# Fetching the first adjacency block in two row groups, and the attention rows in three transfers

## The chip, the core and the metric

The kernel runs on one core of a Trainium2 chip. The core has a matrix engine (TensorE, PE in the profile), VectorE (DVE), ScalarE (ACT), GpSimd (POOL) and SyncE (SP), and 16 DMA engines that move data between the chip's memory and the on-chip buffer. The metric is the device time of one execution in microseconds. The profile that is quoted was taken from one execution; its span runs from the first to the last instruction of the core.

## The reference

The reference is one graph-attention layer with a residual and a layer norm. `x` is 4096 x 512, `adj` is 4096 x 4096, `W` is 512 x 2048 (four heads of 512), `a` holds two vectors of 512 for each head, all in float32.

```
ht      = (x @ W) split into 4 heads
e       = leaky_relu(src_i + dst_j) + adj_ij        # for each head
h_prime = mean over heads of softmax(e) @ ht
out     = layernorm(x + h_prime)
```

`adj` is added as it stands, and its entries reach 1e9. So in almost every row the softmax puts all its weight on the column where `adj` is largest, and `h_prime` of that row is `x[column] @ mean over heads of W`. The kernel computes that, and tests with a bound from the norms of `x`, `W` and `a` that the largest entry leads far enough; rows where it doesn't are done by a general path, which isn't entered for these inputs.

## The kernel before, in words

The 4096 rows are handled as NB = 32 blocks of 128 rows, P = 128 being the number of partitions. Block `ib` holds rows `32*p + ib`, so partition `p` of a block gets one row of 16 KB (4096 floats), and neighbouring partitions read rows that lie 512 KB apart in memory. All of this is in `leading_rows`.

For each block VectorE takes maxima over short segments (`segment_maxima`, L180), finds the leading segment (L187, L189), and GpSimd fetches that segment again with an indirect DMA (L200). Two blocks later VectorE finds the column in it (L217, L223), and GpSimd gathers the row of `x` that belongs to it (L211). Three blocks after the first step TensorE turns this row (L238) and multiplies it by the mean of the heads' weights (L253), adding `x` through an identity matmul (L246). ScalarE takes the statistics and scales (L275, L277, L286), and SP stores.

The order of all instructions is written out by hand (`tc.manual_schedule`). Every large transfer is issued from SP, in program order, on one queue: block 0 of `adj`, half of `W`, block 1, the other half of `W`, blocks 2 to 4, the first rows of `x`. From then on the loop over `t` issues the load of block `t + 5`. The adjacency blocks live in a pool of six buffers (`AHEAD + 1`), so a later load also waits until VectorE has left the buffer of six blocks before.

The four small transfers of `a` (L135) are issued from ScalarE, in front of its first other work. They bring the eight attention vectors, of 2 KB each, to partitions 0 to 7, two rows each time. TensorE turns them (L353) after the first weight blocks have been averaged.

Transfers from SP and ScalarE take turns on eight completion semaphores, which are called lanes here (0 to 7). A transfer that gets a lane waits until the lane's last transfer has landed. Before, the lanes of the first eight transfers are: rows of `a` 0, 2, 3 and 4; block 0 of `adj` 1; first half of `W` 5; block 1 of `adj` 6; second half of `W` 7. So block 2 of `adj` waits for the first transfer of `a`, block 3 for block 0 of `adj`, block 4 and the first rows of `x` for the second and third transfers of `a`, and block 5 for the fourth.

Of the kernel before, what the change touches and what calls it, by code (L numbers as in the profile page):

```python
# [9 lines left out]
F32 = mybir.dt.float32  # L10
# [10 lines left out]
P = 128  # L21
# [9 lines left out]
def gat_resnorm_kernel(  # L31
# [29 lines left out]
    any_bad = keep.tile([1, 1], I32, name="any_bad")  # L61

    leading_rows(tc, x, adj, W, a, out, ident, v, n_bad, any_bad)

    flag = nc.values_load(any_bad[0:1, 0:1], min_val=0, max_val=N)
# [5 lines left out]
def leading_rows(ctx, tc, x, adj, W, a, out, ident, v, n_bad, any_bad):  # L71
# [8 lines left out]
    nc = tc.nc  # L80
    N, D = x.shape
    H = a.shape[0]
# [8 lines left out]
    adj_pool = ctx.enter_context(tc.tile_pool(name="adj_pool", bufs=AHEAD + 1))  # L91
# [7 lines left out]
    adj_rows = adj.rearrange("(p nb) m -> nb p m", nb=NB)  # L99
# [11 lines left out]
    a_rows = once.tile([2 * H, D], F32, name="a_rows")  # L111

    once.tile([P, 32], F32, name="pad_end")
    adj_t = {}

    def pieces(ib):
        return PIECES if ib == NB - 1 else 2 if ib >= LATE else 1

    def load_adj(ib):
        if 0 <= ib < NB:  # L120
            t = adj_t[ib] = adj_pool.tile([P, N], F32, name="adj_t")
            n = pieces(ib)
            for k in range(n):
                nc.sync.dma_start(t[:, ts(k, N // n)], adj_rows[ib][:, ts(k, N // n)])  # L124
# [4 lines left out]
    def load_w(kb, n):  # L129
        nc.sync.dma_start(hold[:, ds(w_at + kb * H, n * H), :], w_blocks[:, ds(kb * H, n * H), :])  # L130

    load_adj(0)
    for s in range(2):
        for h in range(0, H, H // 2):
            nc.scalar.dma_start(  # L135
                a_rows[ds(s * H + h, H // 2), :], a[ds(h, H // 2), ts(s, D), :].rearrange("h d o -> h (d o)")
            )
    for kb in range(0, KB, 2):
        load_w(kb, 2)
        load_adj(kb // 2 + 1)  # L140
# [291 lines left out]
    for t in range(NB):  # L432
# [29 lines left out]
        ib = t - PROJECT  # L462
# [244 lines left out]
```

## Time and profile before

| what | value |
|---|---|
| time, median of 3 runs | 235.2 us (234.88 to 235.32) |
| time of the profiled execution | 234.9 us |
| its span | 233.4 us |
| PE busy | 199.9 us (86%) |
| DVE busy | 191.3 us (82%) |
| ACT busy | 111.8 us (48%) |
| POOL busy | 100.7 us (43%) |
| bytes moved by DMA | 97.12 MB, mean 416 GB/s |
| granted TensorE clock, mean | 0.965 |

Busy time is the time in which an engine executed something; PE and DVE overlap for most of the span. The DMA share is the mean busy share of the 16 DMA engines. The time of an execution lies 1.5 us above its span. Beside the views the trace has a record of every DMA packet, with its queue, start, duration and size; packets of 16,384 bytes are rows of an adjacency block. Where a packet's time is given below, it comes from these records, counted from the span's start.

### The profile page before, as it was taken

How to read it: one execution, taken by the hardware profiler on the slowest of the kernel's cores; microseconds unless marked ns; L12 is line 12 of the kernel's file. 1: busy time of each engine (PE TensorE's matmuls, PEld its weight loads, DVE VectorE, ACT ScalarE, POOL GpSimd, SP SyncE). 2: the span in 40 equal slices, each digit the busy share in tenths (PEclk: the TensorE clock that was granted, in tenths of full speed). 3: DMA queues.
4: the chain of work that ended last, by engine and by line, in shares of the span. 5: the costliest groups of instructions: out<-in, count | busy, mean ns of one | idle time of the engine just before them, and what ended most of it. 6: DMA issues, size and time to landing. Idle time of an engine off the chain costs nothing.

```text
span 233.4 us, 2484 instructions
## 1 busy us (share of the span) xinstructions
PE 199.9 (86%) x683; PEld 105.3 (45%) x683; DVE 191.3 (82%) x300; ACT 111.8 (48%) x267; POOL 100.7 (43%) x215
## 2 busy tenths in 40 slices
PE   0069995999999999999999779879998977999980
PEld 0034644646565555665645244334443433444460
DVE  0548299689929999999788995999999999998881
ACT  2001223014474757575767455545664644188561
POOL 2020234414524464644543452647464564548300
PEclk9999999579999999999999979999999999999997
DMA  6999999999999999999999999999999999999995
GB/s 237 423 432 428 428 438 426 415 439 436 422 421 437 423 431 425 431 419 428 430 430 428 432 423 432 423 430 421 426 433 420 426 423 426 412 424 420 421 414 213
DMA packets 12257, 97.12 MB, mean 416 GB/s; under 512 B 1992, under 2 KB 2440, under 8 KB 6480
## 3 DMA queue, kind: packets, MB, share of 16 engines
q1 hardware_dynamic: 8640, 88.08, 89.1%
q0 software_dynamic: 3584, 8.84, 9.6%
q8 instruction: 6, 0.10, 0.2%
q14 instruction: 11, 0.09, 0.1%
q10 hardware_dynamic: 16, 0.02, 0.0%
HBM read 88.54 MB, written 8.39 MB: 415 GB/s over the span
## 4 chain that ended last, share of the span: by engine, by line
DMA 64%; DVE 21%; PE 11%; SPq 1%; issue 1%; ACT 0%; DVEq 0%
DMA adj_t<-in_adj_dram 53%; DVE seg L180 17%; DMA hold<-in_x_dram 11%; PE o L253 6%; PE o L295 2%; DVE at L189 1%; PE tp L238 1%; DVE top L187 1%; PE o L246 1%; DVE within L223 1%; SPq L130 1%; PE o L291 0%; SPq L124 0%; DVE inner L217 0%; ACT hold L335 0%
## 5 line engine op out<-in xcount | busy, mean ns | idle before, releaser
L180 DVE TENSOR_REDUCE seg<-adj_t 128x128 f32<-128x2048 f32 (+3 forms) x66 | 145.5, 2208 | 28.5 <-DMA adj_t<-in_adj_dram 28.2
L253 PE MATMUL o<-w_sum,yt 128*128 128x512 f32 x248 | 117.6, 616 | 0.7 <-ACT yt L240 0.7
L253 PEld LDWEIGHTS o<-w_sum,yt 128*128 128x128 f32 x248 | 45.6, 196 | 55.2 <-issue 43.9
L240 ACT COPY yt<-tp 128x512 f32<-128x512 f32 x32 | 18.8, 588 | 43.9 <-PE tp L238 43.8
L200 POOL DMA_INDIRECT lead<-in_adj_dram,row x32 | 32.3, 1008 | 14.6 <-POOL row L196 14.6
L211 POOL DMA_INDIRECT y<-in_x_dram,col x32 | 30.9, 964 | 15.4 <-POOL col L225 15.1
L238 PE MATMUL tp<-ident,y 128*128 128x128 f32 x128 | 22.1, 296 | 10.2 <-DMA y<-in_x_dram,col 10.1
L246 PE MATMUL o<-hold,ident 128*128 128x512 f32 x52 | 28.5, 634 | 1.7 <-DMA hold<-in_x_dram 1.7
L343 PE MATMUL o<-hold,ident 128*128 128x512 f32 x32 | 17.3, 696 | 13.6 <-DMA hold<-in_L_gnn_W_dram 13.6
L238 PEld LDWEIGHTS tp<-ident,y 128*128 128x128 f32 x128 | 18.5, 209 | 22.8 <-issue 20.5
L361 ACT COPY wt<-tp 128x512 f32<-128x512 f32 x16 | 9.2, 587 | 38.2 <-PE tp L359 38.2
L196 POOL TENSOR_TENSOR row<-at,first 128x1 uint32<-128x1 uint32 x32 | 6.1, 190 | 43.6 <-DVE at L189 43.6
L367 PEld LDWEIGHTS pv<-at_d,wt 128*128 128x128 f32 x128 | 17.2, 200 | 7.4 <-ACT wt L361 3.7
L260 ACT ACTIVATE sq<-hold 128x512 f32<-128x512 f32 x32 | 19.8, 620 | 0.0
L225 POOL TENSOR_TENSOR col<-start,within 128x1 uint32<-128x1 uint32 x31 | 5.9, 190 | 32.2 <-DVE within L223 32.2
L286 ACT ACTIVATE hold<-o,nm,sd 128x512 f32<-128x512 f32 x24 | 17.2, 771 | 0.0
L277 ACT ACTIVATE sq<-o,nm 128x512 f32<-128x512 f32 x24 | 16.5, 687 | 0.8
L343 PEld LDWEIGHTS o<-hold,ident 128*128 128x128 f32 x32 | 6.9, 225 | 21.5 <-issue 21.5
L367 PE MATMUL pv<-at_d,wt 128*128 128x2 f32 x128 | 16.0, 249 | 0.6 <-ACT wt L361 0.6
L344 ACT ACTIVATE w_sum<-o 128x512 f32<-128x512 f32 x4 | 2.4, 598 | 27.5 <-PE o L343 27.5
L275 ACT ACTIVATE sq<-o 128x512 f32<-128x512 f32 x24 | 14.5, 606 | 0.0
L187 DVE MAX8 top<-seg 128x8 f32<-128x256 f32 (+2 forms) x32 | 11.6, 362 | 1.1
(86 smaller groups left out, 140.0 us busy)
## 6 DMA issues: line engine op xcount, KB each, us to landing
adj_t<-in_adj_dram SPq DMA_DIRECT2D x28, 2048.0 KB, 30.8
adj_t<-in_adj_dram SPq DMA_DIRECT2D x6, 1024.0 KB, 28.1
hold<-in_L_gnn_W_dram SPq DMA_DIRECT2D x2, 2048.0 KB, 16.4
hold<-in_x_dram SPq DMA_DIRECT2D x2, 2048.0 KB, 37.6
out_dram<-hold SPq DMA_DIRECT2D x4, 1024.0 KB, 16.1
out_dram<-hold SPq DMA_DIRECT2D x7, 512.0 KB, 14.4
hold<-in_x_dram SPq DMA_DIRECT2D x3, 1024.0 KB
adj_t<-in_adj_dram SPq DMA_DIRECT2D x4, 512.0 KB, 19.8
```

What stands on the lines that cost most here:

```text
L180: nc.vector.tensor_reduce(seg_of[ib][:, ts(k, N // e // n)], adj_t[ib][:, ts(k, N // n)].rearrange("p (s e) -> p s e", e=e), axis=AX.X, op ...
L200: nc.gpsimd.indirect_dma_start(out=lead, out_offset=None, in_=adj_segs[e], in_offset=bass.IndirectOffsetOnAxis(ap=row[:, :1], axis=0),)
L211: nc.gpsimd.indirect_dma_start(out=y, out_offset=None, in_=x, in_offset=bass.IndirectOffsetOnAxis(ap=col[:, :1], axis=0),)
L238: nc.tensor.transpose(tp[:, kb, :], y[:, ds(kb, P, KB)], ident)
L240: nc.scalar.copy(yt, tp)
L246: nc.tensor.matmul(o_ps[ib], ident, hold[:, ib, :], start=start, stop=False)
L253: nc.tensor.matmul(o_ps[ib], yt_of[ib][:, kb, :], w_sum[:, kb, :], start=(start and kb == 0), stop=(kb == KB - 1),)
L260: nc.scalar.activation(sq, hold[:, ib, :], AF.Square, accum_out=xx[:, ib : ib + 1])
L277: nc.scalar.activation(sq, o, AF.Square, bias=nm[:, i], accum_out=sd[:, i])
L286: nc.scalar.activation(hold[:, ib, :], o_ps.pop(ib), AF.Identity, bias=nm[:, i], scale=sd[:, i])
L343: nc.tensor.matmul(o, ident, hold[:, w_at + kb * H + h, :], start=(h == 0), stop=(h == H - 1))
L367: nc.tensor.matmul(pv[:, kb, h : 2 * H : H], wt[:, k, :], at_d[:, k, h : 2 * H : H], start=(k == 0), stop=(k == KB - 1),)
```

## The change

Block 0 of `adj` is loaded by two transfers, partitions 0 to 15 in the first (256 KB) and partitions 16 to 127 in the second (1792 KB), both from SP and into the same buffer. The rows of `a` come in three transfers, the first of which brings four rows, in place of four transfers of two rows. Two lines are added to the file, so that lines behind L135 have numbers higher by two.

```diff
-    load_adj(0)
-    for s in range(2):
-        for h in range(0, H, H // 2):
-            nc.scalar.dma_start(
-                a_rows[ds(s * H + h, H // 2), :], a[ds(h, H // 2), ts(s, D), :].rearrange("h d o -> h (d o)")
-            )
+    def load_adj_in_parts(ib, *parts):
+        t = adj_t[ib] = adj_pool.tile([P, N], F32, name="adj_t")
+        for lo, hi in zip((0, *parts), (*parts, P)):
+            nc.sync.dma_start(t[lo:hi, :], adj_rows[ib][lo:hi, :])
+
+    load_adj_in_parts(0, P // 8)
+    for s, h, n in ((0, 0, H), (1, 0, H // 2), (1, H // 2, H // 2)):
+        nc.scalar.dma_start(a_rows[ds(s * H + h, n), :], a[ds(h, n), ts(s, D), :].rearrange("h d o -> h (d o)"))
     for kb in range(0, KB, 2):
         load_w(kb, 2)
         load_adj(kb // 2 + 1)
```

SP has one transfer more and ScalarE one less, so the number of transfers on the lanes stays. The lanes become: rows of `a` 0, 2 and 3; block 0 of `adj` 1 (first part) and 4 (second part); everything from the first half of `W` on as before. VectorE's first instruction waits for lanes 1 and 4 in place of lane 1, TensorE's turning of `a` for three lanes in place of four, and the load of block 3 waits for the first part of block 0 alone, that of block 5 for the second part. No other instruction is added, removed or moved on any engine.

## The prediction

> **What bounds the kernel now.** I read the page's slices first, then the windows, because a change in the first microseconds is worth something only if the start carries through to the end. In the slices the row of DMA shares is:
>
> ```profile
> DMA  6999999999999999999999999999999999999995
> GB/s 237 423 432 428 428 438 426 415 439 436 422 421 437 423 431 425 431 419 428 430 430 428 432 423 432 423 430 421 426 433 420 426 423 426 412 424 420 421 414 213
> ```
>
> Only the first and last of 40 slices are not full. The DMA engines never rest between; 97.12 MB at about 426 GB/s is 228 us of a span of 233.4. No other engine is as full (PE 86%, DVE 82%). The chain of waits agrees: from 107.84 us on, it alternates between transfers and short work, and ends in a load of `x`, behind which TensorE runs without a break.
>
> ```profile
> 107.84 34.79 DMA adj_t<-in_adj_dram
> ...
> 147.42 28.81 DMA adj_t<-in_adj_dram
> ...
> 176.29 25.22 DMA hold<-in_x_dram
> 201.51 0.04 issue
> 201.55 1.98 PE o L246 x4
> ```
>
> These DMA pieces run from issue to landing, and most of each is time behind other transfers in the queue. So what the stream of bytes loses or gains in its first 10 us reaches the load of `x` at 201.5, and the end with it. Then I looked at the start in narrow windows (the last two columns are DMA share and GB/s):
>
> ```profile
> 0.00:2.00 2.00, 0.00 (x0) 0.00 (x0) 0.00 (x0) 0.00 (x0) 1.06 (x10) 1.00 0.05 10
> 2.00:3.00 1.00, 0.00 (x0) 0.00 (x0) 0.00 (x0) 0.42 (x1) 0.38 (x6) 1.00 0.95 246
> 3.00:4.00 1.00, 0.00 (x0) 0.00 (x0) 0.00 (x0) 0.86 (x1) 0.00 (x0) 1.00 0.77 328
> 4.00:5.00 1.00, 0.00 (x0) 0.00 (x0) 0.00 (x0) 0.00 (x0) 0.00 (x0) 1.00 0.92 393
> ```
>
> and in the order of SP's and ScalarE's issues:
>
> ```profile
> 0.98 0.39 SPq L124 DMA_DIRECT2D adj_t<-in_adj_dram  x1
> 1.06 1.49 ACTq L135 DMA_DIRECT2D a_rows<-in_L_gnn_a_dram  x4
> ...
> 1.42 0.43 SPq L130 DMA_DIRECT2D hold<-in_L_gnn_W_dram  x1
> ```
>
> SP issues block 0 at 0.98. By the packet records the 16 engines start their first row between 1.995 and 2.894 us (mean 2.59) and end it between 3.300 and 3.957 (mean 3.62). From then on every row takes 0.611 us on its engine, one each 0.607. Block 0 has landed on the first engine at 7.56 and on the last at 8.22, and VectorE starts at 8.67. The staggered start of 0.90 us is what the change can touch.
>
> [...] two-row transfers of `a` have two completion packets each, 128-row ones 16. [...]
>
> **The change part by part.**
>
> *One issue more on SP.* An issue takes 0.33 to 0.44 us there when nothing holds it up, so the first half of `W` is issued at about 1.85 in place of 1.42. It is hidden: the engines have block 0 to move until 8, and each 2 MB behind it takes 4.9 us more. Without that queue it would cost 0.4.
>
> *One issue less on ScalarE.* Four took 1.49 us, so about 0.3 less. ScalarE then loads a table (1.28 us) and waits 16.2 us for its first matmul: nothing. The bytes of `a` are the same 16 KB. TensorE uses them at 20.0 us; they had landed by 8.9.
>
> *Waits.* VectorE's first reduction waits for both parts; behind it on VectorE stands its whole program, and GpSimd's first lookup, which has 11.9 us of idle time. This wait ends with the later part, and is priced below. SP's load of block 3 waited until 8.67 for block 0 and can now go at about 5; what is queued behind it (block 4, `x`, block 5) goes earlier or at the same time. Nothing is gained, because 8 MB stand ahead of block 3. If the second part is late, block 5 is issued late by as much, with over 20 us of queue ahead of it: nothing.
>
> *The earlier start of all engines.* 128 rows took 0.90 us to reach all engines, 7 ns a row, so 16 rows take 0.11. The first row starts at 2.0 as before (1.01 us after its issue), all have started by 2.1, mean 2.05: 0.54 us earlier than 2.59. The second part is issued at about 1.4, its rows arrive from 2.4 to 3.2, while first rows take at least 0.76 us (the shortest seen), so a gap is at most 0.3 on the last engines. The early starters before took 1.2 to 1.48 us for their first row, and if that is the cold start and not the stagger, rows end at 3.3 at best, 0.32 before the mean of 3.62. So a gain of 0.3 to 0.54 from this alone.
>
> [...]
>
> *The second part.* 112 rows are seven for each engine, 4.25 us at 0.607. Which row goes to which engine the trace doesn't show. [...] 0 to about 1.2 us (two rows of 0.61), of which I take 0.5. [...]
>
> *Sum.* 1.37 + 0.5 is 1.9 us on 234.9 for the profiled execution, 236.8. The median shown stands 0.3 above that execution, so I say 237.0 for the median. This case's own range is 235.8 [...] to 238.8 [...].
>
> **The rivals.** *Only the earlier start* (the other side). [...] For it: the second and third pairs of `a` rows[...] overlap at 6.11 and 6.14 us and take 84 ns each, with no stretch; but these are 2 KB each. [...] A landing waits for the slowest engine, whose first row ended at 3.957 and could end at 3.3, so the gain lies between 0.3 and 0.65: 234.5 to 234.9, and four fifths of this case lie beyond the 0.2% line.
>
> *No change at the end.* The engines don't end together: completion packets of one transfer spread over 0.65 us until 40 us, over 1.45 after a 16 KB instruction fetch held one engine at 42.65, over 2.45 at 178.7. A transfer lands with its slowest engine; if that is one that started early before and was held up later, the gain does not pass on: 235.2.
>
> *The second part in lockstep[...]*[...], about 249.
>
> *A wait in place of the one removed.* VectorE begins at about 10.5 instead of 8.67. It has 17.1 us of waits for loads in the first 40 us, so a delay of 2 has cover and the bytes alone decide: the same 237.
>
> **How the numbers follow.** Case one (ports, 237.0) 0.52; earlier start alone 0.34; no change 0.08; lockstep 0.06; the changed wait gives case one's number and has its chance in it. Within 0.2% (0.47 us) is about what a measurement of this kernel can tell from no change. Faster is four fifths of 0.34, 0.27; same is the rest of it and the case of no change, 0.15; slower is case one and lockstep, 0.58. The range goes from 234.6, which takes in nearly all of the earlier start, to 238.9, the end of case one; lockstep is left out.
>
> **What would show it.** Right: the packet records show first rows that start within 0.2 us of each other and last 2 us or more; the windows from 2 to 5 us show 100 to 150 GB/s in place of 246 to 393; VectorE starts at 10 or later; after 15 us the slices are as before, only moved by 2 us. Wrong: first rows of 0.8 to 1.2 us and VectorE's start at 8.1 to 8.4, with the load of `x` landing before 201.5. It would also be wrong if the DMA share fell below full in the middle, which would mean that the bytes are not the bound.

## The result, and the profile after

The changed kernel takes 238.53 us in the median (238.36 to 238.71), the kernel before 235.22. The ratio is 1.0144 with a 95% interval of 1.0126 to 1.0161: 3.3 us slower. The profiled execution has a span of 236.9 us, 3.5 more than before. The forecast, 237.0 us, had the sign and the kind of loss, and 1.8 us of its 3.3.

The slices of the page of after, to be laid beside those of before:

```profile
DMA  6999999999999999999999999999999999999994
GB/s 140 308 429 427 429 441 411 431 439 417 432 425 427 426 436 419 434 430 418 432 430 426 430 426 428 424 423 429 432 425 428 418 425 427 409 426 418 425 406 191
```

The first two slices have changed, 140 and 308 GB/s in place of 237 and 423, and from the third to the last but one nothing beyond a few per cent. The row of shares alone would not show it: the second digit is 9 in both. The engines were busy, but with slower rows. That is the first thing to read here: the same share of 9 stands beside 423 GB/s in one run and 308 in the other.

The windows of the first 12 us of after (DMA share and GB/s in the last two columns):

```profile
2.00:4.00 2.00, 0.00 (x0) 0.00 (x0) 0.00 (x0) 1.28 (x1) 0.37 (x6) 1.00 1.47 266
4.00:6.00 2.00, 0.00 (x0) 0.00 (x0) 0.00 (x0) 0.00 (x0) 0.00 (x0) 1.00 0.64 182
6.00:8.00 2.00, 0.00 (x0) 0.00 (x0) 0.00 (x0) 0.00 (x0) 0.00 (x0) 1.00 1.08 322
8.00:10.00 2.00, 0.00 (x0) 0.00 (x0) 0.00 (x0) 0.00 (x0) 0.00 (x0) 1.00 1.03 287
10.00:12.00 2.00, 0.00 (x0) 0.00 (x0) 0.15 (x1) 0.00 (x0) 0.00 (x0) 1.00 0.83 270
12.00:14.00 2.00, 0.00 (x0) 0.00 (x0) 2.00 (x1) 0.00 (x0) 0.00 (x0) 1.00 1.03 442
```

and the same windows of before:

```profile
2.00:4.00 2.00, 0.00 (x0) 0.00 (x0) 0.00 (x0) 1.28 (x1) 0.38 (x6) 1.00 0.86 287
4.00:6.00 2.00, 0.00 (x0) 0.00 (x0) 0.00 (x0) 0.00 (x0) 0.00 (x0) 1.00 0.92 393
6.00:8.00 2.00, 0.00 (x0) 0.00 (x0) 0.00 (x0) 0.00 (x0) 0.00 (x0) 1.00 1.04 446
8.00:10.00 2.00, 0.00 (x0) 0.00 (x0) 1.33 (x1) 0.00 (x0) 0.00 (x0) 1.00 1.00 428
10.00:12.00 2.00, 0.00 (x0) 0.00 (x0) 2.00 (x2) 0.00 (x0) 0.00 (x0) 1.00 1.03 442
```

Between 4 and 12 us the same queue moves 182 to 322 GB/s and not 393 to 446, and the full rate comes back at 12, when block 0 is through. The share in a short window can exceed 1 (1.47 from 2 to 4 us), as a packet is counted where it begins. The packet records give the loss row by row. From 4 to 16 us 16 rows are in progress at once, as many as there are engines, in 89% of the time before and 90% after. A packet's record doesn't name its engine, so the rows are put in order of time here and taken 16 at a time, one for each engine. Row 1 is the first part, rows 2 to 8 are the second, row 9 is the first of `W`:

| row | mean end before, us | mean end after, us | behind by, us |
|---|---|---|---|
| 1 | 3.62 | 3.51 | -0.11 |
| 2 | 4.23 | 5.11 | 0.88 |
| 3 | 4.85 | 6.03 | 1.18 |
| 5 | 6.07 | 7.84 | 1.77 |
| 8 | 7.91 | 10.58 | 2.67 |
| 9 | 8.53 | 11.56 | 3.03 |
| 10 | 9.14 | 12.19 | 3.05 |

From row 11 on a row takes 0.611 us again and nothing is regained. The first half of `W` has landed on its last engine at 16.06 in place of 13.08, 2.98 later; the fourth transfer behind it (block 3) at 35.57 in place of 32.59, again 2.98; the fifth transfer from the end at 230.29 in place of 227.24, 3.05 later. In between the transfers land 2.8 to 3.6 us later, and in the mean of the 16 engines 3.0 to 3.2. So a delay of the first 12 us is carried nearly unchanged to the end. VectorE starts at 11.85 in place of 8.67. The chain of waits of after ends in loads too, then in TensorE's last products:

```profile
167.54 25.57 DMA adj_t<-in_adj_dram
193.11 0.01 issue
193.13 17.35 DMA adj_t<-in_adj_dram
...
215.22 5.29 DMA lead<-in_adj_dram,row
...
226.50 3.55 PE o L297 x16
```

The loads are other ones than in the chain of before: the last of `adj` and the fetch of a segment (`lead`), with VectorE's short work between, in place of the load of `x` at 201.5. But that load is late by as much. TensorE's first product behind it, for which it waited, starts at 204.87 in place of 201.55, and from there TensorE works on, with one pause of 0.16 us. Its last products end 3.3 us later than before (230.05, before 226.76).

### The profile page after: what moved, and what is told of

Its sections match the earlier page's. It is cut to its first block, busy times and chain, and to the rows that moved or that the text cites. A ratio compares the mean times of both kernels' runs of the same rounds, so it can differ in the third digit from the quotient of the medians.

```text
span 236.9 us, 2484 instructions
## 1 busy us (share of the span) xinstructions
PE 198.1 (84%) x683; PEld 103.9 (44%) x683; DVE 191.0 (81%) x300; ACT 111.7 (47%) x267; POOL 100.4 (42%) x215
## 3 DMA queue, kind: packets, MB, share of 16 engines
q0 software_dynamic: 3584, 8.84, 9.4%
## 4 chain that ended last, share of the span: by engine, by line
DMA 74%; DVE 18%; PE 4%; SPq 1%; issue 1%; ACT 0%; DVEq 0%
DMA adj_t<-in_adj_dram 72%; DVE seg L182 14%; DMA lead<-in_adj_dram,row 2%; PE o L255 2%; PE o L297 1%; DVE col L233 1%; DVE at L191 1%; DVE top L189 1%; DVE within L225 1%; SPq L130 0%; SPq L135 0%; DVE inner L219 0%; PE tp L240 0%; ACT hold L337 0%; DVE halves_st L331 0%
## 5 line engine op out<-in xcount | busy, mean ns | idle before, releaser
L255 PEld LDWEIGHTS o<-w_sum,yt 128*128 128x128 f32 x248 | 45.0, 194 | 54.3 <-issue 42.8
L345 PE MATMUL o<-hold,ident 128*128 128x512 f32 x32 | 16.6, 673 | 16.6 <-DMA hold<-in_L_gnn_W_dram 16.6
L248 PE MATMUL o<-hold,ident 128*128 128x512 f32 x52 | 27.6, 617 | 1.5 <-DMA hold<-in_x_dram 1.5
L189 DVE MAX8 top<-seg 128x8 f32<-128x256 f32 (+2 forms) x32 | 11.6, 361 | 1.1
```

What stands on the lines that cost most here:

```text
L248: nc.tensor.matmul(o_ps[ib], ident, hold[:, ib, :], start=start, stop=False)
L255: nc.tensor.matmul(o_ps[ib], yt_of[ib][:, kb, :], w_sum[:, kb, :], start=(start and kb == 0), stop=(kb == KB - 1),)
L345: nc.tensor.matmul(o, ident, hold[:, w_at + kb * H + h, :], start=(h == 0), stop=(h == H - 1))
```

## The experiments

Two theories stood at the start. Ports, as in the prediction, is my name for a supposition: which partitions a transfer writes sets how fast its rows go. The runs show rates and the times of rows; a port shows in none of them. The row times that the expectations draw from it ahead of the runs (1.22 us for the halves, 2.44 for parts of 16) are my estimates; 1.288 and 2.02 to 2.06 were measured. The other: the loss comes from what else changed, the small first transfer on a cold start, the second issue, the waits or the lanes. Each diff below is against the changed kernel, the last one against the kernel before; `...` marks what is left out. Each loss is against executions of the kernel before that were taken together with the run (medians of 234.97 to 235.10 us).

**The two halves of the change.** The split alone, with the rows of `a` in four transfers:

```diff
-    for s, h, n in ((0, 0, H), (1, 0, H // 2), (1, H // 2, H // 2)):
-        nc.scalar.dma_start(a_rows[ds(s * H + h, n), :], ...)
+    for s in range(2):
+        for h in range(0, H, H // 2):
+            nc.scalar.dma_start(a_rows[ds(s * H + h, H // 2), :], ...)
```

> Only the split of block 0 at partition 16 is kept; the rows of a come in four transfers as before, so the lanes of all later transfers move by one. Port theory [...]: the loss is all here, 3.0 to 3.6 us slower than before, about 238.5. Lane theory (the loss comes from the changed waits between transfers and from the order of the a rows): a good part of the 3.3 us goes, 236 or less.

Measured: 238.76 us, ratio 1.0153 (1.0136 to 1.0170), 3.7 us slower, slightly above the 3.6 that I gave as the end. The reverse, three transfers of `a` and block 0 in one:

```diff
-    load_adj_in_parts(0, P // 8)
+    load_adj(0)
```

> Only the rows of a in three transfers; block 0 is one transfer of 128 rows. Port theory: as before, within 0.4 us of it. Lane theory: 1 us or more slower than before.

Measured: 235.25 us, ratio 1.0006 (0.9997 to 1.0015). The whole loss is the split's. The lanes don't matter: with them moved by one it is 3.7 us, with them kept 3.3, and the intervals overlap.

**The split at partition 64.**

```diff
-    load_adj_in_parts(0, P // 8)
+    load_adj_in_parts(0, P // 2)
```

> As the change, but the split is at partition 64, so each part gives every engine four rows in place of one and seven. Port theory: [...] every row takes about 1.22 us, and block 0 needs 9.8 us in place of 4.9: 4 to 5 us slower than before, more than the change. Start theory (a small first transfer is what hurts: a cold start, a second issue, two waits): no worse than the change, and less the less the first part is small, so under 3 us.

Measured: 240.10 us, ratio 1.0213 (1.0196 to 1.0230), 5.0 us slower than before. Two equal large parts cost more than a small and a large one, and the packet records show rows of 1.288 us where the halves run undisturbed (the means of rows 3, 7 and 8), against 0.611. Windows of this run:

```profile
6.00:8.00 2.00, 0.00 (x0) 0.00 (x0) 0.00 (x0) 0.00 (x0) 0.00 (x0) 1.00 0.78 172
8.00:10.00 2.00, 0.00 (x0) 0.00 (x0) 0.00 (x0) 0.00 (x0) 0.00 (x0) 1.00 1.20 248
10.00:12.00 2.00, 0.00 (x0) 0.00 (x0) 0.00 (x0) 0.00 (x0) 0.00 (x0) 1.00 0.90 188
```

About 200 GB/s while the rows of block 0 are loaded: half the rate. A small first transfer is not needed for the loss.

**The split by columns.**

```diff
-        for lo, hi in zip((0, *parts), (*parts, P)):
-            nc.sync.dma_start(t[lo:hi, :], adj_rows[ib][lo:hi, :])
+        for lo, hi in zip((0, *parts), (*parts, N)):
+            nc.sync.dma_start(t[:, lo:hi], adj_rows[ib][:, lo:hi])
 
-    load_adj_in_parts(0, P // 8)
+    load_adj_in_parts(0, N // 8)
```

> As the change, but block 0 is split by columns: the first 512 columns of all 128 partitions (256 KB, the bytes of the change's first part), then the other 3584. The same number of transfers, the same waits and lanes. Port theory: [...] the loss goes: within 0.6 us of before. Start theory: as slow as the change, about 3.3 us slower than before.

Measured: 235.25 us, ratio 1.0009 (1.0000 to 1.0018). Issues, waits, lanes and the bytes of both parts are the change's; only all 128 partitions are in each part, and the loss is gone. Windows of this run:

```profile
4.00:6.00 2.00, 0.00 (x0) 0.00 (x0) 0.00 (x0) 0.00 (x0) 0.00 (x0) 1.00 1.09 455
6.00:8.00 2.00, 0.00 (x0) 0.00 (x0) 0.00 (x0) 0.00 (x0) 0.00 (x0) 1.00 1.08 460
```

It also tells something of the earlier start. All 16 engines are at work at once for the first time at 2.66 us, in place of 2.89 before, and block 0 has landed on its last engine at 8.08 in place of 8.22. At the end of the kernel nothing of these 0.14 us is to be seen. The start isn't even here either: at 2.40 us only 9 packets are in progress, though 21 of 2 KB have begun.

**The same split on `W`.** Block 0 in one transfer; the first half of `W`, which comes second in the queue, split at partition 16.

```diff
     def load_w(kb, n):
-        nc.sync.dma_start(hold[:, ds(w_at + kb * H, n * H), :], w_blocks[:, ds(kb * H, n * H), :])
+        for lo, hi in ((0, P // 8), (P // 8, P)) if kb == 0 else ((0, P),):
+            nc.sync.dma_start(hold[lo:hi, ds(w_at + kb * H, n * H), :], w_blocks[lo:hi, ds(kb * H, n * H), :])
 ...
-    load_adj_in_parts(0, P // 8)
+    load_adj(0)
```

> Block 0 of adj is whole; in its place the first half of W, the second transfer of the queue, is split at partition 16 (rows of a in three transfers, so the number of transfers on the lanes is the change's). Every partition reads 16 KB here too, but its rows lie 32 KB apart in memory, not 512 KB, and the engines are already running. Port theory (write side, by partition): the same loss as the change, 2.7 to 3.7 us slower than before, with rows of W of 0.8 to 1.6 us. Memory theory (the parts read rows 512 KB apart in an unlucky order) or start theory: within 0.6 us of before.

Measured: 240.33 us, ratio 1.0222 (1.0199 to 1.0244), 5.2 us slower. So the cause is neither the cold start nor the way the rows of `adj` lie in memory. Windows of this run:

```profile
6.00:8.00 2.00, 0.00 (x0) 0.00 (x0) 0.00 (x0) 0.00 (x0) 0.00 (x0) 1.00 1.32 403
8.00:10.00 2.00, 0.00 (x0) 0.00 (x0) 0.09 (x1) 0.00 (x0) 0.00 (x0) 1.00 1.02 123
10.00:12.00 2.00, 0.00 (x0) 0.00 (x0) 2.00 (x1) 0.00 (x0) 0.00 (x0) 1.00 0.76 131
12.00:14.00 2.00, 0.00 (x0) 0.00 (x0) 2.00 (x2) 0.00 (x0) 0.00 (x0) 1.00 1.05 279
14.00:16.00 2.00, 0.00 (x0) 0.00 (x0) 1.31 (x4) 0.00 (x0) 0.19 (x1) 1.00 0.99 254
```

The last line of these stands for the large part, the second and third for the small one. VectorE starts at 9.91 here, only 1.24 us later than before, and the kernel still loses 5.2: the bytes decide, not VectorE's first wait. But 5.2 is above what I expected, 2.7 to 3.7. Within a running stream the small part holds up three rows of each engine (means of 1.60, 2.05 and 1.30 us, 3.1 more than three rows of 0.611), at the start of the kernel only one (1.60). And the rows of the large part take 0.96 to 1.04 us here, 0.84 to 0.97 in the change. The first rows of a cold stream are slow anyway (1.03 us before), which may cover a part of the loss; that is not shown. Why the large part's rows are slower than those of `adj`, no run shows.

**Eight parts of 16.**

```diff
-    load_adj_in_parts(0, P // 8)
+    load_adj_in_parts(0, *range(P // 8, P, P // 8))
```

> Block 0 in eight transfers of 16 partitions, the rows of a in three. Port theory: [...] 2.44 us for each in place of 0.61, 19.5 for the block in place of 4.9: 14 to 15 us slower than before[...]. [...] the parts would overlap in part: 5 to 10. Issue theory (each transfer more costs its share): at most 3 us.

Measured: 246.69 us, ratio 1.0494 (1.0476 to 1.0512), 11.6 us slower: between the two ranges that I gave for ports, 5 to 10 and 14 to 15, and far above the 3 for issues. From the fourth part on a row takes 2.02 to 2.06 us in the mean of the engines, with hardly any spread (2.01 to 2.08). Windows of this run:

```profile
8.00:10.00 2.00, 0.00 (x0) 0.00 (x0) 0.00 (x0) 0.00 (x0) 0.00 (x0) 1.00 1.04 131
10.00:12.00 2.00, 0.00 (x0) 0.00 (x0) 0.00 (x0) 0.00 (x0) 0.00 (x0) 1.00 1.05 131
12.00:14.00 2.00, 0.00 (x0) 0.00 (x0) 0.00 (x0) 0.00 (x0) 0.00 (x0) 1.00 0.98 123
```

256 KB in 2.055 us is 128 GB/s, where a row of 0.611 us on each engine, one each 0.607, is 429 to 432. Eight times the 1.44 us that such a row takes beyond 0.611 is 11.5, about the whole loss.

**The large part first.**

```diff
-    load_adj_in_parts(0, P // 8)
+    load_adj_in_parts(0, P - P // 8)
```

> As the change with the parts in the other order: partitions 0 to 111 in the first transfer, 112 to 127 in the second. It tells whether the large part is slow by itself or only behind the small one. Port theory [...]: the 112 rows are slow by themselves, 0.8 to 1.0 us a row from the second row on, and the kernel is 1.7 to 3.5 us slower than before. If only the small part costs: rows of 0.61 in the large part, and about 1 us slower than before.

Measured: 238.77 us, ratio 1.0154 (1.0133 to 1.0175), 3.7 us slower, a little above the 3.5 that I gave as the end for ports. Rows 2 to 7, all of the large part and with nothing but itself ahead, have means of 0.78 to 1.01 us and take 1.75 us more in all than six rows of 0.611. So the 112 rows are slow by themselves. The small part behind them brings two rows of 1.56 and 1.60 us.

**Which partitions, with everything else equal.** Eight transfers of 16 partitions again, but every eighth one:

```diff
-        for lo, hi in zip((0, *parts), (*parts, P)):
-            nc.sync.dma_start(t[lo:hi, :], adj_rows[ib][lo:hi, :])
+        for j in range(8):
+            nc.sync.dma_start(t[j : P : 8, :], adj_rows[ib][j : P : 8, :])
```

> Block 0 in eight transfers of 16 partitions as in the run with eight parts, but each takes every eighth partition (j, j+8, ..., j+120) in place of 16 neighbours. Transfers, bytes, engines and lanes are the same[...]. Port theory: 1.29 us for each transfer, as in the halves, in place of 2.06, and about 5 us slower than before (4.5 to 6). If a transfer of 16 partitions is slow whichever they are, or the memory side sets it (its rows lie further apart here, 4 MB): as the eight neighbouring parts, 11.6 us slower, or more.

Measured: 240.65 us, ratio 1.0259 (1.0225 to 1.0293), 5.7 us slower in place of 11.6. Windows of this run:

```profile
8.00:10.00 2.00, 0.00 (x0) 0.00 (x0) 0.00 (x0) 0.00 (x0) 0.00 (x0) 1.00 0.98 205
10.00:12.00 2.00, 0.00 (x0) 0.00 (x0) 0.00 (x0) 0.00 (x0) 0.00 (x0) 1.00 1.02 213
```

The number of transfers, their bytes and the one row per engine are those of the eight neighbouring parts, and the rate is 205 to 238 GB/s in place of 107 to 131. In memory the rows lie further apart, 4 MB, which doesn't explain a faster load; that the distance isn't what sets the rate is also seen in the small part of `W`, whose rows lie 32 KB apart and took 2.05 us, as the neighbouring parts of `adj` do with rows 512 KB apart. Which partitions are written together is left; why 16 neighbours are slower than every eighth partition, no run shows. Last, four parts of 32:

```diff
-    load_adj_in_parts(0, P // 8)
+    load_adj_in_parts(0, 32, 64, 96)
```

> Block 0 in four transfers of 32 neighbouring partitions, two rows for each engine. Port theory: [...] as the two halves: 1.29 us a row and 4.5 to 5.5 us slower than before, though there are twice as many transfers as in the halves. If the number of parts sets the loss: between the halves (5.0) and the eight parts (11.6), about 7.

Measured: 240.38 us, ratio 1.0225 (1.0208 to 1.0242), 5.4 us slower, with rows of up to 1.28 us in the mean: nearly as the halves, with twice the transfers.

**What staggers the start.** Block 0 whole, the rows of `a` from SP behind the first half of `W`:

```diff
     load_adj(0)
-    for s in range(2):
-        for h in range(0, H, H // 2):
-            nc.scalar.dma_start(...)
     for kb in range(0, KB, 2):
         load_w(kb, 2)
+        if kb == 0:
+            for s in range(2):
+                nc.sync.dma_start(a_rows[ds(s * H, H), :], a[:, ts(s, D), :].rearrange("h d o -> h (d o)"))
         load_adj(kb // 2 + 1)
```

> Block 0 whole; the rows of a come in two transfers of four rows from SP behind the first half of W, so that nothing is issued from ScalarE while block 0's rows are handed to the engines. If the stagger of the first rows comes from the issues of a in between, the start is closed up and the kernel is 0.2 to 0.5 us faster than before. If the cold first rows set the start, as the split by columns suggests: within 0.3 us of before.

Measured: 235.45 us, ratio 1.0015 (1.0008 to 1.0022). The first rows start between 2.012 and 3.115, no closer together than before, so the issues of `a` in between are not what staggers them. What staggers them stays open. Block 0 lands 0.16 us earlier, and yet the kernel is 0.35 slower, just outside the 0.3 that I gave; what takes that back was not traced. No run points to a kernel that is faster than before.

## Why the prediction was right, and where it was off

*The bytes bound the kernel, and a loss in the first microseconds reaches the end.* Right, nearly one to one: 2.98 us behind at 16 us, 3.3 in the medians. In the seven other runs that split by partitions the first half of `W` has landed later than 13.08 by 3.0 (16 and 112, `a` in four), 3.3 (112 first), 4.2 (four parts), 4.5 (halves), 4.9 (strided), 5.2 (`W`) and 10.8 (eight parts), and the medians are slower by 3.7, 3.7, 5.4, 5.0, 5.7, 5.2 and 11.6: they follow this delay, with up to 1.2 us more that arises later and was not traced.

*Issues, waits and lanes cost nothing.* Right, as far as the runs can tell: the three transfers of `a` give a ratio of 1.0006, and the split by columns, with the change's issues and waits, 1.0009. SP issued block 3 earlier, as said, and it brought nothing. VectorE's later start (11.85, 3.18 us later) can't be told from the delay of the bytes in this run, as both come to about 3 us; in the split of `W` it is 1.24 of 5.2, and there the bytes decide.

*The earlier start, 0.3 to 0.54 us.* Too high. I had all first rows begin within 0.11 us, by 2.1; they began between 2.012 and 2.654, at 2.22 in the mean and not 2.05. And their mean end moved by 0.11 only; how much of this is the small part's own slowness was not shown. The run with only the rows of `a` changed has no split: there the first rows began 0.28 us earlier in the mean, lasted 1.16 in place of 1.03, ended 0.16 earlier, and block 0 landed at 8.21, where before had 8.22. The engines that start first have long first rows (1.2 to 1.5 us before), and most of an earlier start is lost in them. The rival that rested on this gain falls for that reason as well as for the slow rows behind the first. (Its evidence for quick writes was loosely told: the packets at 6.11 and 6.14 us are the two rows of the second pair of `a`, and those of the third come at 7.41 and 7.44.)

*The first part, 1.37 us net of the earlier start.* The 1.37 in the sum is my estimate of what the first part's rows lose; it rested on a rate for 16 partitions that no trace of before shows. The rows are slow, as said; the size at the start was 0.88, the lag after row 2. From the mean start of 2.05 that I assumed, the 0.42 us that a first row took beyond 0.611 before (3.62 less 2.59 less 0.61) and the 2.055 us that such a row takes in the run with eight parts follows an end at 4.52, 0.90 after 3.62; as the start wasn't the one that I assumed, that this comes so close is in part chance. My signs for it were wrong in detail: I expected first rows that begin within 0.2 us of each other and last 2 us or more, and 100 to 150 GB/s from 2 to 5 us; the windows show 266 and then 182. The first rows lasted 1.29 us, shorter than 2.06, and it was the rows behind them that were long (1.60 in the mean, 1.95 at most). So a part of the cost comes with the next row; the first row of `W` behind the eight parts, which goes to all partitions, shows the same (1.61 us). How the cost passes on is not in the records. In a stream that is already running the same part costs 3.1.

*The second part, 0.5 us.* This is the term of the sum that was mis-sized. From row 2 to row 9 it cost 2.15 us (0.88 to 3.03), over four times what I took and beyond the 1.2 that I gave as its usual end. I let at most two rows cost double, an estimate with nothing of the trace of before behind it but the 0.61 us of a row. The runs show that every row costs: each of the rows 3 to 8 lost 0.23 to 0.36 us, and the first row of `W` behind them another 0.36. The run with the large part first shows that the loss is its own. Why it is so large stays open. The trace doesn't name a packet's engine, so how the rows are shared out was not seen. The lockstep rival, about 249 for the kernel, is excluded: its 13 to 14 us more stand against 3.3.

*The sum.* -0.11 to row 1, 0.99 more to row 2, 2.15 more to row 9 make 3.03, where I had 1.9; the rest, up to the 3.3 of the medians, arises behind and was not traced. That the time lies inside the range, 0.4 us under its upper end, owes something to luck: the first part's term was taken too large and the second part's far too small, and the two errors worked against each other.

## What to carry to other kernels

When the queue is full and a large load has to be split, split it by columns and not by partitions: here two transfers of a 2 MB block cost nothing one way (512 and 3584 columns, the one cut that was tried) and 3 to 5 us the other. What counted here is which partitions are written at the same time, not how many transfers there are: of 429 to 432 GB/s block 0 kept about half in two halves (172 to 248), four quarters (rows of up to 1.28 us in place of 0.611) or eight strided parts (205 to 238) alike, and under a third in eight neighbouring parts (107 to 131). And when a part is added to a stream that bounds the kernel, look at the rows behind it as well as at the part.

## What the runs showed of the hardware that I had not expected

Sixteen neighbouring partitions take 128 GB/s in a running stream (256 KB in 2.055 us), where all 128 take 429 to 432. A load of 112 of 128 partitions, which leaves out one eighth, runs at about 290 GB/s by itself (16 rows in 0.90 us, rows 2 to 7 of the run with the large part first), two thirds of the rate. The same split of `W` costs 5.2 us in second place of the queue, against 3.3 for block 0 at its head. And of the 16 completion packets behind the change's first part 14 took 27 to 38 ns, in place of 9 before.
